# One 128-row load per image row, or two of 63 and 64 rows: the neighbourhood tiles of an involution and ternary convolution block

## The chip, the cores and the metric

The kernel runs on one core of one Trainium2 chip. The metric is the device time of a run in microseconds. Each time given for a kernel is the median of its runs; the kernel before has 2163.08 us as the median of three runs (2159.76 to 2169.76).

## The reference

The input x is 8 images of 256 channels, 56 x 56, in float32. Two layers follow, each added to its input.

```
x = x + involution(group_norm(x))      # 7x7 kernels made from x itself, 16 groups
x = x + block(group_norm(x))           # two 3x3 ternary convolutions, batch norms, ReLU

involution:  ker = w_span @ (w_reduce @ x + b_reduce) + b_span     # 16 x 49 per pixel
             out[c, y, x] = sum over 49 taps of ker[group(c), tap, y, x] * x_padded[c, y + i, x + j]
block:       out1 = relu(bn(conv(x, q1) + center));  out2 = bn(conv(out1, q2) + center)
             relu(out1 + out2),   q = weights quantized to -1, 0, 1
```

The change is in the involution, in the loads of the padded x that the 49 taps are taken from.

## The kernel before, in words

The kernel works in three stages. The first (to about 1043 us) is the involution with its group norm, the second (to about 1880 us) is the two convolutions, and the third is the closing pass over the results. The change is in the first.

In the first stage the 256 channels are split into four quarters of 64, and the image into an upper and a lower half, so that 128 partitions hold 64 channels of both halves. An image quarter is worked through in ten rows (TY = 10); a row is three image lines (the last one: one line) of seven tiles of 8 pixels. So there are 8 x 4 x 10 = 320 rows, and the stage is a list of them, in one order.

For each row there is a neighbourhood tile q. The host lays the padded image out in x_nb so that, for each quarter, one line of 896 values (3584 bytes: seven tiles by 128 channel halves) belongs to one position of a window of 9 x 14 = 126 positions (NQ). q holds 128 such lines, one per partition; 126 of them are read.

- `load_q` (L726) takes a buffer of the pool q (NQB = 5 buffers) and issues the load on SP, from 128 lines of x_nb in one DMA (L729).
- `fill_rim` (L746, its operation recorded at L752) adds the group's mean at the rim of the padded image, on POOL.
- `fill_end` (L761, L765) overwrites the lines below the image, on ACT, in the last two rows of a quarter.
- `apply_row` (L836, L853) multiplies q, on TensorE, by the matrices a that `generate` made for this quarter: 56 small matmuls (28 in the last row), out into the PSUM tile pa, which has two buffers.
- `pick_out` scales pa into inv on ACT (L863) and DVE (L865), and adds inv to x on POOL (L869).

Between the rows stand the pieces of the next quarter's `generate` (matmuls L821, ACT L825, DVE L829), the loads of the next image (`load_x`, L611), the stores of finished quarters (`store_x1`, L890), the statistics (L150), and the quantization of the convolution weights, which loads pieces (L221, L296) and stores planes (L325). All of these DMAs are issued on SP, in the order of the text.

Order: row i runs `apply_row`, then `prefetch` issues the load of row i + 5 (its buffer has just been read for the last time), then come the statistics and `pick_out`, then `surround` runs `fill_rim` of row i + 3 and `fill_end` of row i + 2. So a load has two rows until its rim is filled, and five until it is read. The function `pin` fixes the order of the text on each engine within the first stage. The second stage isn't pinned: its first instructions (the loads raw at L353 and wq at L342, the normalization xp at L1050 and L1052, the planes p, q, r, u, v at L388 to L416, the casts pl at L393) are placed by the scheduler of the framework, also among the last rows of the first stage. The convolution matmuls are at L523. The framework also gives each DMA one of eight semaphores in turn, and puts in the waits.

Of the kernel before, what the change touches and what calls it, by code (L numbers as in the profile page):

```python
# [17 lines left out]
P = 128  # L18
# [17 lines left out]
PY, PX = 3, 8  # L36
# [4 lines left out]
QY, QX = PY + K - 1, PX + K - 1  # L41
# [6 lines left out]
HQ = TY * PY + K - 1  # L48
# [42 lines left out]
def involution_tri_block_kernel(  # L91
# [3 lines left out]
    nc = tc.nc  # L95
# [484 lines left out]
    with ExitStack() as ph1:  # L580
# [121 lines left out]
        for j in range(2):  # L702
            o = j * nf // 2
# [22 lines left out]
        def load_q(b, c, ty):  # L726

            q = qpool.tile([P, TX, P], F32, tag="q", name=f"q_{b}_{c}_{ty}")
            nc.sync.dma_start(q.rearrange("p k c -> p (k c)"),  # L729
                              x_nb[b, c, (HQ - QY - PY * ty) * QX:(HQ - QY - PY * ty) * QX + P, :])  # L730
            return q

        def rim_of(b, c):
# [141 lines left out]
        def prefetch():  # L875
            if queue:
                k = queue.pop(0)
                loads[k] = load_q(*k)
                bare.append(k)
# [200 lines left out]
    with ExitStack() as ph4:  # L1080
# [10 lines left out]
        for j in range(B * CT):  # L1091
            b, t = j // CT, j % CT
# [98 lines left out]
```

## Time and profile before

| | us |
|---|---|
| median of three runs | 2163.08 |
| lowest, highest | 2159.76, 2169.76 |
| the profiled execution | 2159.04 |
| its span, from first to last instruction | 2157.3 |

The page's busy shares and its 40 slices (54 us each; a digit is the busy share in tenths):

```profile
PE 1748.1 (81%) x29680; PEld 1619.6 (75%) x29680; DVE 1751.9 (81%) x3337; ACT 1436.7 (67%) x3553; POOL 588.1 (27%) x965
...
PE   4898898989989898998799999997999999960000
...
DVE  5787878787777878777799999998999999984444
ACT  3877686877868787787366666665666666653344
POOL 0565565555556656566200000000000000000000
...
DMA  5667678686767768577633333335323333369999
```

The first 19 or 20 slices are the involution: all five engines and the DMA engines work side by side. The middle is the convolutions, with TensorE and DVE nearly full, and the last five are the closing pass, which moves data. The busiest DMAs by the page, with what each moves and the time from issue to landing (the last number, in us):

```profile
q<-in_x_nb SPq DMA_DIRECT2D x320, 448.0 KB, 4.1
...
x<-in_x SPq DMA_DIRECT2D x64, 392.0 KB, 5.2
x1d<-x SPq DMA_DIRECT2D x64, 392.0 KB, 5.3
```

### The profile page before, as it was taken

To read this page: it belongs to the slowest core of one execution; us is meant where nothing else is said; L and a number is where in the kernel's file an instruction comes from. 1 tells how busy PE (TensorE), PEld (TensorE's weight loads), DVE (VectorE), ACT (ScalarE), POOL (GpSimd) and SP (SyncE) were. 2 spreads that over 40 slices of the span, in tenths; PEclk is the share of its full clock that TensorE was granted. 3 is DMA by queue.
4 is the path that set the end of the run, shared out by engine and by line. 5 is a ranking of instruction groups with operands and counts; after the bars stand their busy time and mean duration, and the time that the engine had idled before them with its cause. 6 is when DMAs were issued, how large, how long until landed. Compare 5 with 4: busy or idle time off the path is not lost.

```text
span 2157.3 us, 70705 instructions
## 1 busy us (share of the span) xinstructions
PE 1748.1 (81%) x29680; PEld 1619.6 (75%) x29680; DVE 1751.9 (81%) x3337; ACT 1436.7 (67%) x3553; POOL 588.1 (27%) x965
## 2 busy tenths in 40 slices
PE   4898898989989898998799999997999999960000
PEld 4777786867777687876699999997999999960000
DVE  5787878787777878777799999998999999984444
ACT  3877686877868787787366666665666666653344
POOL 0565565555556656566200000000000000000000
PEclk9999899999999999999799999998999999985555
DMA  5667678686767768577633333335323333369999
GB/s 184 219 189 235 191 220 244 182 261 187 252 193 223 240 181 272 176 206 215 235 122 122 122 122 122 122 122 204 116 108 126 127 127 127 123 261 426 429 428 395
DMA packets 156250, 440.06 MB, mean 204 GB/s; under 512 B 63774, under 2 KB 74012, under 8 KB 148508
## 3 DMA queue, kind: packets, MB, share of 16 engines
q1 hardware_dynamic: 150336, 405.50, 55.3%
q10 hardware_dynamic: 5596, 30.03, 3.4%
q8 instruction: 235, 3.85, 0.7%
q14 instruction: 83, 0.68, 0.1%
HBM read 323.28 MB, written 112.20 MB: 202 GB/s over the span
## 4 chain that ended last, share of the span: by engine, by line
PE 69%; DMA 10%; issue 7%; DVE 6%; POOL 5%; ACT 3%; SPq 0%; ACTq 0%; POOLq 0%; DVEq 0%
PE c L523 40%; PE pg L821 15%; PE pa L853 9%; DMA x1f<-x1d 4%; PE pk L714 3%; DMA y1f<-y1d 3%; POOL q L752 2%; DMA out_y<-x1f 2%; POOL x L869 2%; PE ks L787 1%; ACT a L825 1%; DVE x1f L1103 1%; POOL x L801 1%; DVE a L829 1%; DMA sums<-in_w_all 1%
## 5 line engine op out<-in xcount | busy, mean ns | idle before, releaser
L523 PE MATMUL c<-pl,wq 128*128 128x392 f32 x4608 | 857.3, 349 | 14.4 <-ACT pl L393 14.4
L523 PEld LDWEIGHTS c<-pl,wq 128*128 128x128 f32 x4608 | 855.4, 190 | 16.1 <-ACT pl L393 14.8
L825 ACT ACTIVATE a<-pg,bt 126x126 f32<-126x126 f32 (+1 forms) x2048 | 537.4, 474 | 95.5 <-PE pg L821 94.0
L821 PE MATMUL pg<-kr,wl 64*126 64x140 f32 (+1 forms) x6144 | 464.8, 295 | 27.7 <-issue 13.2
L821 PEld LDWEIGHTS pg<-kr,wl 64*126 64x126 f32 x6144 | 401.4, 197 | 55.9 <-issue 19.0
L853 PE MATMUL pa<-a,q 126*32 126x48 f32 x17024 | 291.8, 214 | 80.4 <-issue 70.4
L853 PEld LDWEIGHTS pa<-a,q 126*32 126x32 f32 x17024 | 240.2, 115 | 148.2 <-issue 99.8
L829 DVE TENSOR_TENSOR a<-pg,bt 126x504 f32<-126x504 f32 (+4 forms) x640 | 282.3, 480 | 43.3 <-PE pg L821 41.9
L869 POOL TENSOR_TENSOR x<-x,inv 128x168 f32<-128x168 f32 x320 | 166.0, 519 | 403.5 <-DVE inv L865 357.5
L865 DVE SCALAR_TENSOR_TENSOR inv<-pa,gn1s,inv 128x168 f32<-128x168 f32 (+1 forms) x384 | 134.6, 351 | 167.0 <-ACT inv L863 163.3
L393 ACT CAST pl<-r 128x812 fp32r<-128x812 f32 x192 | 162.3, 868 | 142.8 <-DVE r L388 123.7
L373 POOL MEMSET xp<- 128x116 f32 x32 | 6.3, 195 | 825.7 <-DVE a L388 825.7
L752 POOL TENSOR_TENSOR q<-q,sides 126x256 f32<-126x256 f32 (+1 forms) x320 | 224.9, 703 | 2.1 <-PE pa L853 1.7
L394 DVE TENSOR_TENSOR pl<-r,pl 128x812 fp32r<-128x812 f32 x192 | 186.6, 998 | 29.9 <-ACT pl L393 28.6
L458 ACT ACTIVATE dummy<-y,nc 128x1568 f32<-128x1568 f32 (+1 forms) x128 | 200.2, 1564 | 4.8 <-DVE y L543 3.5
L863 ACT ACTIVATE inv<-pa,gn1s 128x168 f32<-128x168 f32 x320 | 135.5, 424 | 72.7 <-PE pa L853 53.8
L150 DVE BATCH_NORM_STATS2 st<-x 128x6 f32<-128x392 f32 x256 | 137.8, 554 | 10.4 <-DMA x<-in_x 9.4
L801 POOL TENSOR_TENSOR x<-x,add 128x504 f32<-128x504 f32 (+1 forms) x128 | 126.3, 1017 | 24.1 <-ACT add L795 24.1
L1050 ACT ACTIVATE xp<-raw,gn 128x392 f32<-128x392 f32 (+1 forms) x124 | 82.5, 721 | 61.3 <-DVE a L388 58.8
L1070 ACT ACTIVATE xp<-raw,bi_bn,sc_bn 128x392 f32<-128x392 f32 (+1 forms) x124 | 82.3, 721 | 58.8 <-DVE a L388 57.1
L1101 DVE SCALAR_TENSOR_TENSOR y1f<-y2f,sc_bn,y1f 128x3136 f32<-128x3136 f32 (+2 forms) x20 | 56.6, 2831 | 63.9 <-DMA y2f<-y2d 49.4
L714 PE MATMUL pk<-x,wrn 64*128 64x168 f32 (+1 forms) x1152 | 99.1, 312 | 2.1 <-issue 2.1
(174 smaller groups left out, 1776.7 us busy)
## 6 DMA issues: line engine op xcount, KB each, us to landing
q<-in_x_nb SPq DMA_DIRECT2D x320, 448.0 KB, 4.1
raw<-x1d SPq DMA_DIRECT2D x32, 812.0 KB, 6.1
raw<-y1d SPq DMA_DIRECT2D x32, 812.0 KB, 7.1
x<-in_x SPq DMA_DIRECT2D x64, 392.0 KB, 5.2
x1d<-x SPq DMA_DIRECT2D x64, 392.0 KB, 5.3
y1d<-y SPq DMA_DIRECT2D x30, 784.0 KB, 3.8
y2d<-y SPq DMA_DIRECT2D x30, 784.0 KB, 3.4
y1f<-y1d SPq DMA_DIRECT2D x14, 1568.0 KB, 15.1
```

Of the source, the lines that this page charges most:

```text
L393: nc.scalar.copy(hi, r)
L394: nc.vector.tensor_tensor(lo, r, hi.bitcast(F32), ALU.subtract)
L458: nc.scalar.activation(dst, v, f, bias=shift[:, to:to + 1], accum_out=stats[:, to, j, n:n + 1])
L523: nc.tensor.matmul(ps[:, to, :NM], wq[k][:, t, dx, to * P:(to + 1) * P], part[:, t, :, dx:dx + W], start=(c == 0), stop=(c == last))
L714: nc.tensor.matmul(ps[h][:, :m * W], wrn[rows, c, :], src[rows, r0:r0 + (m - 1) * PY + 1:PY, :], start=(c == 0), stop=(c == NCQ - 1))
L752: nc.gpsimd.tensor_tensor(v, v, z, ALU.add)
L801: nc.gpsimd.tensor_tensor(x_, x_, v, ALU.add)
L821: nc.tensor.matmul(dst, wl[rows, c, gp, o:o + NQ], kr[py][rows, px, :], start=True, stop=True)
L825: nc.scalar.activation(dst[:, g + 1, p0 + j], ps[1][:NQ, j * nt + t0:j * nt + t1], AF.Identity, bias=bt[:, c, g + 1, p0 + j:p0 + j + 1])
L829: nc.vector.tensor_tensor(dst[:, g, p0:p0 + n].rearrange("q p t -> q t p"), ps[0][:NQ, t0 * n:t1 * n].rearrange("q (t p) -> q t p", p=n), ...
L853: nc.tensor.matmul(ps[o:o + m, k * w:(k + 1) * w], q[:NQ, k, o:o + m], av[:, t + k, g * w:(g + 1) * w], start=True, stop=True)
L869: nc.gpsimd.tensor_tensor(xv, xv, iv.rearrange("p t (y x) -> p y t x", x=PX), ALU.add)
```

## The change

The load of a neighbourhood tile is issued as two DMAs, one behind the other on SP: the first brings lines 0 to 62 to partitions 0 to 62, the second lines 63 to 126 to partitions 63 to 126. Line 127, which was loaded before and which no instruction reads, is no longer loaded. Everything else in the text is the same.

```diff
         def load_q(b, c, ty):
 
             q = qpool.tile([P, TX, P], F32, tag="q", name=f"q_{b}_{c}_{ty}")
-            nc.sync.dma_start(q.rearrange("p k c -> p (k c)"),
-                              x_nb[b, c, (HQ - QY - PY * ty) * QX:(HQ - QY - PY * ty) * QX + P, :])
+            o = (HQ - QY - PY * ty) * QX
+            for p0, p1 in ((0, 63), (63, 127)):
+                nc.sync.dma_start(q[p0:p1].rearrange("p k c -> p (k c)"), x_nb[b, c, o + p0:o + p1, :])
             return q
 
```

## The prediction

> **What bounds the kernel now.** I read the page's busy shares and slices first, then the two stages by windows, the waits of the first stage, the DMA queues, what waits on the q loads, and the row-by-row timeline of the seam between the stages. All q loads lie in the first 1043 us; the rest is the convolutions (1043 to 1880 us) and the closing pass, which the diff doesn't touch. The first stage by windows, and the DMA queues in the same window:
>
> ```profile
> 60.00:1040.00 980.00, 856.53 (x24622) 732.81 (x24622) 763.55 (x2119) 751.08 (x2656) 576.08 (x919) 0.95 0.72 218
> ```
> ```profile
> DMA packets 119967, 213.75 MB, mean 218 GB/s; under 512 B 58336, under 2 KB 68064, under 8 KB 119714
> ...
> q8 instruction: 194, 3.18, 1.4%
> ...
> q<-in_x_nb SPq DMA_DIRECT2D x315, 448.0 KB, 4.1
> ```
>
> Columns of the first: window, length, busy us of PE, PEld, DVE, ACT, POOL, TensorE clock, DMA share, GB/s. TensorE works 857 of 980 us (87%); DVE and ACT follow at 78% and 77%; the DMA engines are busy 72% of the time. A row takes 980/315 = 3.1 us. What makes up TensorE's 123 idle us is in the waits of this window:
>
> ```profile
> PE pa L853 <- issue: 70.4, 66, 3.0
> ...
> PE pg L821 <- issue: 13.2, 12, 3.0
> ...
> PE pa L853 <- POOL q L752: 6.1, 2, 5.7
> ```
>
> The reader is to see that 70.4 + 13.2 = 84 us in 78 waits have no semaphore behind them ("issue"). In the trace's packet records most of these gaps end 1.2 to 1.6 us after the end of a 16,384-byte packet of the instruction queue (for example a packet at 602.20 to 603.09 us, matmuls again at 604.67). I read them as TensorE waiting for its own instructions[...]. Waits for q itself are 6 us, in two places. The q loads' own view in this window, what their first reader on POOL (L752) waited for, and SP's waits over the whole span:
>
> ```profile
> DMA to landing us min/median/max: 3.0/4.1/6.8
> ```
> ```profile
>   DMA q<-in_x_nb: 0.3, 1
> ```
> ```profile
> SPq L729 <- PE pa L853: 658.8, 301, 34.6
> ```
>
> One wait of 0.3 us in 320 rows: the loads are hidden. SP, which issues them, idles 659 us until TensorE frees a buffer. The seam is different:
>
> ```profile
> 1037.52 0.72 POOL L752 TENSOR_TENSOR q<-q,sides 126x256 f32<-126x256 f32 x1 [1.72 <-PE pa L853]
> ...
> 1038.28 0.56 ACT L765 COPY q<-low 70x448 f32<-70x448 f32 x1 [1.88 <-POOL q L752]
> ...
> 1039.66 2.99 PE L853 MATMUL pa<-a,q 126*32 126x48 f32 x84 [2.26 <-POOL x L869]
> ...
> 1040.70 1.75 DVE L1052 TENSOR_SCALAR xp<-raw,gn 128x392 f32<-128x392 f32 x4
> ...
> 1044.41 0.57 DVE L150 BATCH_NORM_STATS2 st<-x 128x6 f32<-128x392 f32 x1 [0.41 <-POOL x L869]
> ...
> 1051.26 1.00 DVE L415 TENSOR_TENSOR u<-xp 128x812 f32<-128x812 f32 x1
> ```
>
> The last q load lands at 1037.36 by the trace's landing records and POOL takes it at 1037.52: there the load is on the path.
>
> [...] Of before's DMAs 824 of 826 show 16 landing increments[...]; none here has 63 rows. [...] the x loads (128 partitions, 392 KB) land in 5.2 us, the x1 stores (64 partitions, 392 KB) in 5.3. [...]
>
> **The change part by part.**
>
> *Bytes.* Row 127, which nothing reads (the kernel uses 126), is dropped: 1/128 of the load. Nothing.
>
> *Engine shares.* [...] q is 315 x 448 KB = 145 of 214 MB, two thirds. [...]
>
> *When q lands.* An undisturbed q packet takes 0.14 us in the packet records. [...] the second issue adds its 0.33 us if the engines are otherwise free. Against that one disturbed row: a small transfer issued right behind q (0.38 us later) stalls on SP by 0.24 to 0.48 us on average, by up to 2.1 us at worst. Estimate from these: +0.7 us typically, +2 in bursts. The cover: by the landing records, the fill at L752 starts 4.3 us after landing at the median (1.2 at the lowest fiftieth), and TensorE reads the row another 5.2 us after the fill (median; 0.7 at least). Added row by row, 2 us makes 19 fills late by 14 us in all, and none reaches TensorE; nor does 3 us. Cost on the path: 0. Without this cover the 320 rows would cost 0.7 us each, 224 us.
>
> *SP.* 320 more issues of 0.33 us and 0.27 us of stalls each, some 190 us, out of 659 idle. What is queued behind each: the next x loads, x1 stores and weight pieces, all early by microseconds. The program has eight DMA semaphores in turn, so each issue waits for the landing of the eighth DMA before it. Before, the nearest of these is 2.0 us clear; with the halves counted, I find some 20 issues held back, 13 us in all, never over 2.3: again inside the cover. 0.
>
> *TensorE's waits.* Each row's first matmul waits for both halves. In the built program TensorE has 975 instructions that only wait, in place of 803, and POOL 548 in place of 388. One takes 51 ns on TensorE's sequencer (L853): 172 x 51 ns = 8.8 us at most. But the sequencer runs ahead: at 606.71 it handles the wait of a row whose matmuls start at 607.77. It costs only where the sequencer is late, 78 of 320 rows or fewer: between 0 and 8.8, I take 1 us. POOL's 160 at 17 ns are inside its idle 40%.
>
> *The seam.* The last load's landing passes through L752 (0.72), the copy at L765 (0.56), and the scaling ops queued behind it on ACT and DVE to the last three rows: +0.7 us. Past it, the built program's order differs. Before, four xp ops on DVE (1.75 us) stand ahead of the last two rows' ops; now they stand among and behind them, and u (1.00 us) stands ahead of the r that ACT and then TensorE wait for. Two xp ops between the last row's three (0.88), one behind the statistics (0.44), and u (1.00): +2.3 us before the first convolution matmul (1050.47 before). From there TensorE is the bound, so it stays. Between 0 (DVE waits hide it) and 3.5; I take 3.0 for landing and order together.
>
> *Instruction fetch.* The unknown. Fetches take 1.4% x 16 x 980 / 194 = 1.13 us each, the quickest tenth 0.90[...]. [...] No trace shows which engine it is. I take 0 and keep both ends.
>
> Sum: 1 + 3 = +4 us on the profiled execution's 2159.0 (span 2157.3 and 1.7 around it), 2163. The runs' median is 2163.1, 4 above that execution; on it, 2167.
>
> **The rivals.**
>
> *Slower by the fuller engines.* [...] each of the 78 waits grows by 0.2 us: +16, with the seam 2183; with all fetches +39, 2206. It decides from 0.09 us per wait, where 7 + 4 us pass 0.5%. For it: [...] 84 us already lost there. Against: half of the fetches run near their quickest time.
>
> *Faster by the emptier engines.* The same coin's other side: -16 + 4 gives 2151. [...] Against: other engines (ACT 77%, DVE 78%) soon hold TensorE.
>
> *The loads don't spread.* Were the 63 rows on one engine, 63 x 0.14 = 8.8 us per row against a pitch of 3.1: 320 x 5.7 us more, near 4000. [...]
>
> *SP's stalls* reach TensorE only from some 5 us per load; a row in ten late by 1 us would be +32, 2199.
>
> **How the numbers follow.** About 0.5%, 11 us, is what a measurement of this kernel can tell from no change. Forecast (hidden, +4): 0.60, 2157 to 2174. Fuller engines: 0.24, nearly all slower. Emptier: 0.12, most of it faster. Not spread: 0.02. SP: 0.02. Faster 0.12, same 0.61, slower 0.27. The range 2150 to 2192 leaves out the far end of the fuller engines' case and the last two.
>
> **What would show it.** Right: q's landing median (last half) 4.6 to 5.2 us; L752 waits for DMA under 15 us in all; TensorE's "issue" waits at L853 and L821 still 70 to 100 us; the first convolution matmul 2 to 5 us later. The fuller engines: mean fetch above 1.3 us and "issue" waits above 100; the emptier: below 1.05 and 70. The forecast is wrong if "PE pa <- POOL q" grows past 20 us, or if the landings double.

## The result and the profile after

The changed kernel takes 2190.1 us (median of four runs, 2180.8 to 2194.8), the kernel before beside it 2165.2: a ratio of 1.0111, 95% interval 1.0068 to 1.0153. On another chip, with 16 runs, it is 2178.8 against 2160.5, ratio 1.0081 (1.0062 to 1.0101). So the change costs 18 to 25 us. That is inside the predicted range, but +4 was forecast, and what the prediction called likeliest (no difference that can be measured) did not happen.

From the page of the changed kernel (the load now stands at L731, and what follows it one line lower than before), profiled in an execution of 2188.5 us:

```profile
span 2186.3 us, 71399 instructions
...
PE 1761.0 (81%) x29680; PEld 1631.5 (75%) x29680; DVE 1747.8 (80%) x3337; ACT 1438.5 (66%) x3553; POOL 589.2 (27%) x965
...
q8 instruction: 235, 3.85, 0.7%
...
L753 POOL TENSOR_TENSOR q<-q,sides 126x256 f32<-126x256 f32 (+1 forms) x320 | 225.2, 704 | 23.8 <-DMA q<-in_x_nb 17.5
```

DVE, ACT and POOL did the same work in the same time, but TensorE was busy for 1761 us where it had 1748, with the same 29680 matmuls. POOL's fill at L753 now does wait for its loads. The first stage by windows, then TensorE's and POOL's waits in it (pg is the PSUM tile of `generate`), then SP's over the whole span:

```profile
60.00:1060.00 1000.00, 865.42 (x24424) 740.01 (x24428) 756.97 (x2113) 748.60 (x2651) 571.65 (x911) 0.94 0.74 210
```
```profile
PE pa L854 <- issue: 65.8, 56, 4.6
...
PE pg L822 <- issue: 27.5, 15, 3.6
...
POOL q L753 <- DMA q<-in_x_nb: 25.3, 20, 2.6
...
PE pa L854 <- POOL q L753: 6.6, 2, 5.6
```
```profile
SPq L731 <- PE pa L854: 450.2, 257, 34.1
```

The reader is to see three things. POOL waits 25 us for q, in 20 places, but what reaches TensorE through "POOL q" is the same 6.6 us as before (6.1). "Issue", which I read as TensorE's wait for its instructions, is 93 us in sum where it was 84, in fewer and longer waits. And SP still has 450 us to spare.

Although so little comes through "POOL q", the loads no longer stay off the path. The page's chain of work that ended last (followed back from the last instruction, at each step to what released it), by engine, first before, then changed:

```profile
PE 69%; DMA 10%; issue 7%; DVE 6%; POOL 5%; ACT 3%; SPq 0%; ACTq 0%; POOLq 0%; DVEq 0%
```
```profile
PE 64%; DMA 13%; issue 10%; POOL 7%; DVE 5%; ACT 2%; SPq 0%; POOLq 0%; ACTq 0%; DVEq 0%
```

Within the first stage this chain goes through loads of q for 59 us in the changed kernel and 9 us in a second profile of it; before, for 4 us and, in its second profile, for none. The chain counts a load from its issue to its landing, so these times are not the loss itself.

Nearly all of the loss is in the first stage. From the first to the last row's scaling on ACT it lasts 1008.1 us; before, 980.7 in its first profile and 983.2 in a second. Everything behind that is 1114.7 us, against 1114.5 and 1115.4. Split up, with a second profile of either kernel (us, differences to the mean of the two profiles of before):

| first stage | before, two profiles | after | after, again |
|---|---|---|---|
| length | 980.7, 983.2 | 1008.1 (+26.1) | 990.1 (+8.1) |
| TensorE busy | 857.1, 857.4 | 868.6 (+11.4) | 859.4 (+2.2) |
| TensorE idle, "issue" | 86.6, 85.2 | 94.0 (+8.1) | 88.8 (+2.9) |
| TensorE idle, all else | 37.0, 40.6 | 45.5 (+6.7) | 41.9 (+3.1) |
| time at half clock | 109, 109 | 140 | 126 |

(A half-clock stretch that begins in the stage is counted to its end, which adds 11 to 13 us to every figure.) So the time went in parts of like size. Of "all else" after the change, 4.7 and 5.0 us are one wait for DVE's scaling just ahead of the last row; before has a gap of 3.5 and 5.0 us at that place, of which 1.3 and 5.0 are booked under "issue". The two profiled executions of the changed kernel (on two chips) differ by 18 us in this stage, those of before by 2.5. Two profiles of each are few: in all, 45 runs of before on one chip lie between 2146 and 2177 us, 16 of the changed kernel on that chip between 2169 and 2186.

The busy part goes with the clock: at the full clock a matmul of this stage stands for 33 to 34 ns of busy time in both kernels, at half clock for 51 to 58. Windows of the changed kernel, each the length of one slot of the clock's records (in both kernels every stretch of this stage between two changes lasts a whole number of 3.41 us; columns as in the windows above, the clock is the third number from the end):

```profile
89.70:93.10 3.40, 3.40 (x142) 3.13 (x131) 2.72 (x7) 3.40 (x18) 3.40 (x5) 1.00 0.84 238
93.10:96.50 3.40, 1.22 (x60) 0.85 (x58) 3.29 (x12) 1.80 (x10) 1.17 (x3) 1.00 0.88 282
96.50:99.90 3.40, 3.40 (x57) 3.13 (x49) 3.40 (x10) 2.33 (x10) 2.37 (x6) 0.51 0.89 289
99.90:103.30 3.40, 2.01 (x76) 1.69 (x72) 2.81 (x9) 1.38 (x6) 1.75 (x4) 0.99 0.78 219
```

In the second window TensorE stood still for 2.2 of 3.4 us; in the third it gets half the clock and does 57 matmuls in the time of 142. There are 26 such half-clock stretches in the stage (24 in the second profile), before 21 and 18. All 26 follow a slot in which TensorE was busy for at most 63% of the time, and every slot at full clock that was busy for less than 46% was followed by one. In the 14 profiles of this document together the two figures are 76% and 46%; in between, both happen. In 15 and 13 of the changed kernel's slots ahead of a stretch most of the idle time is behind an instruction fetch (before 10 and 12); in the others TensorE waits most often for ACT's copies at L826 or for the statistics (L166), and a wait for q takes part in one of either profile. In the second window above a slot that was busy for 36% was enough. Its stall of 2.2 us was paid for once more in the third, by some 1.5 us (an estimate: the third window's 57 matmuls, at the 33 ns of the full clock, would be 1.9 of its 3.4 us).

### The profile page after: what moved, and what is told of

The parts are those of the page before. It is cut to its first block, busy times and chain, and to the rows that moved or that the text cites. A ratio compares the mean times of both kernels' runs of the same rounds, so it can differ in the third digit from the quotient of the medians.

```text
span 2186.3 us, 71399 instructions
## 1 busy us (share of the span) xinstructions
PE 1761.0 (81%) x29680; PEld 1631.5 (75%) x29680; DVE 1747.8 (80%) x3337; ACT 1438.5 (66%) x3553; POOL 589.2 (27%) x965
## 2 busy tenths in 40 slices
DMA packets 158813, 438.95 MB, mean 201 GB/s; under 512 B 66654, under 2 KB 76892, under 8 KB 151068
## 4 chain that ended last, share of the span: by engine, by line
PE 64%; DMA 13%; issue 10%; POOL 7%; DVE 5%; ACT 2%; SPq 0%; POOLq 0%; ACTq 0%; DVEq 0%
PE c L523 39%; PE pg L822 12%; PE pa L854 7%; DMA q<-in_x_nb 3%; POOL q L753 3%; PE pk L714 3%; DMA y1f<-y1d 3%; DMA out_y<-x1f 3%; DMA y2f<-y2d 2%; POOL x L802 2%; PE ks L788 1%; POOL x L870 1%; DVE x1f L1104 1%; DMA x1f<-x1d 1%; ACT a L826 1%
## 5 line engine op out<-in xcount | busy, mean ns | idle before, releaser
L826 ACT ACTIVATE a<-pg,bt 126x126 f32<-126x126 f32 (+1 forms) x2048 | 539.3, 476 | 115.0 <-PE pg L822 114.3
L822 PE MATMUL pg<-kr,wl 64*126 64x140 f32 (+1 forms) x6144 | 474.1, 298 | 42.5 <-issue 27.5
L822 PEld LDWEIGHTS pg<-kr,wl 64*126 64x126 f32 x6144 | 410.1, 200 | 71.4 <-issue 34.6
L753 POOL TENSOR_TENSOR q<-q,sides 126x256 f32<-126x256 f32 (+1 forms) x320 | 225.2, 704 | 23.8 <-DMA q<-in_x_nb 17.5
L394 DVE TENSOR_TENSOR pl<-r,pl 128x812 fp32r<-128x812 f32 x192 | 186.5, 996 | 27.4 <-ACT pl L393 26.1
```

The lines of the kernel that those rows point to most:

```text
L394: nc.vector.tensor_tensor(lo, r, hi.bitcast(F32), ALU.subtract)
L753: nc.gpsimd.tensor_tensor(v, v, z, ALU.add)
L822: nc.tensor.matmul(dst, wl[rows, c, gp, o:o + NQ], kr[py][rows, px, :], start=True, stop=True)
L826: nc.scalar.activation(dst[:, g + 1, p0 + j], ps[1][:NQ, j * nt + t0:j * nt + t1], AF.Identity, bias=bt[:, c, g + 1, p0 + j:p0 + j + 1])
```

## Experiments

The theories at the start: *late data* (the halves land too late for POOL's fill), *rows* (an instruction fetch waits behind q's rows in a DMA engine, longer in a fuller one), *second transfer* (issues, semaphores, waiting instructions). They are guesses of mine. For each kernel I took from the trace two things. The first is the stalls of TensorE behind a fetch: gaps over 0.3 us that end 1.0 to 1.75 us after an instruction packet, up to 1075 us. The second is the wait of a fetch, from the start of instruction 192 of a block of 256 to the start of the packet, in blocks with 169 to 224 matmuls and weight loads of L853. The 60,166 recorded TensorE instructions make the 235 packets at 256 to a packet. The place 192 is where the record meets the edge of a block: 65 of the 68 stalls before, and 58 of the 65 after the change, come at instruction 193 or 194, so they do belong to the fetches. In the table, ratio is to the kernel before on the same chip; the stage is the first one as above; times are in us. All but the ratio comes from one profiled execution of each kernel, and a mean wait, of some 116 fetches, is uncertain by about 0.15 us. Counted to the end of the stage and no further, the stalls are 80 us in the first profile of before, 115 with 126 lines, 88 with 63 + 63 and 138 with the 64-byte transfer, and within 1 us of the table elsewhere.

| kernel | ratio (95%) | stage | stalls behind fetches | wait of a fetch | half clock | POOL's fill waits for q |
|---|---|---|---|---|---|---|
| before | 1 | 980.7 | 83.7 | 2.32 | 109 | 0.3 |
| before again | 1.0001 (0.9983–1.0018) | 983.2 | 83.5 | 2.32 | 109 | 2.4 |
| changed | 1.0111 (1.0068–1.0153) | 1008.1 | 88.8 | 2.49 | 140 | 25.3 |
| changed again | 1.0081 (1.0062–1.0101) | 990.1 | 80.8 | 2.25 | 126 | 11.4 |
| 64 + 64 lines | 1.0222 (1.0193–1.0252) | 1028.1 | 115.0 | 2.73 | 154 | 10.2 |
| one of 126 lines | 1.0210 (1.0174–1.0245) | 1018.0 | 109.8 | 2.67 | 147 | 5.9 |
| 63 + 63 lines | 1.0294 (1.0257–1.0331) | 1041.2 | 85.3 | 2.40 | 191 | 80.1 |
| changed, later fill | 1.0154 (1.0131–1.0177) | 1009.0 | 73.7 | 2.00 | 154 | 2.5 |
| 112 + 16 lines | 1.0161 (1.0102–1.0220) | 1023.1 | 107.0 | 2.59 | 157 | 6.4 |
| before + a 64-byte transfer | 1.0302 (1.0243–1.0362) | 1044.3 | 133.2 | 3.05 | 126 | 7.9 |
| one of 112 lines | 1.0103 (1.0044–1.0161) | 1006.9 | 69.8 | 2.02 | 154 | 2.4 |
| one of 64 lines | 1.0130 (1.0088–1.0172) | 1014.8 | 22.2 | 1.12 | 307 | 0 |
| pieces, 6/7 of the bytes | 0.9929 (0.9901–0.9958) | 967.8 | 69.6 | 2.04 | 106 | 1.6 |
| weights stored flat | 1.0006 (0.9990–1.0023) | 973.0 | 79.4 | 2.18 | 109 | 1.8 |

**Even halves, one odd load, nine engines.** How a transfer is spread shows in its packets of four bytes. Before has 13,343 of them for 826 DMAs, 16 to each (but for 128 that are the data of b_red), and 824 of the DMAs show 16 landing increments. By the packets under 512 bytes (63,774 before) a load of 128 lines has 16 of them and so have loads of 112 (63,774), 64 (63,775) and 16 lines (68,894 with the 112 + 16), one of 126 lines has 14 (63,135), and one of 63 has 9 (66,654 in the changed kernel). I take each for the share of one of the 16 DMA engines that the page counts. That makes 8, 7, 4, 1, 9 and 7 rows to an engine. It is an estimate, since no packet in the trace names its engine; all numbers of rows and of engines below rest on it.

Three divisions of the load, in place of (0, 63), (63, 127): eight rows on each of 16 engines in two transfers; nine rows on 14 engines in one; fourteen rows on nine engines in two.

```diff
-            for p0, p1 in ((0, 63), (63, 127)):
+            for p0, p1 in ((0, 64), (64, 128)):
+            for p0, p1 in ((0, 126),):
+            for p0, p1 in ((0, 63), (63, 126)):
```

> Two transfers of 64 and 64 lines in place of 63 and 64[...], with the same number of DMAs and of waits as in the changed kernel. If the uneven load of the engines[...] makes the changed kernel slower: about 2165 us, within 6 of the kernel before. If the second DMA of each row, its issue on SP and the second wait on TensorE and POOL make it slower: about 2190 us, as the changed kernel.

> One transfer of 126 lines: [...] one DMA and one wait per row as before. Uneven load: [...] some +8 us, 2173. Number of DMAs and waits: 2165 us, no change. [...]

> Two transfers of 63 lines: [...] DMAs and waits as in the changed kernel. Uneven load: [...] at least twice the loss, +50 us or more, 2215 or above, with q landing later than in the changed kernel. Number of DMAs and waits: 2190 us, as the changed kernel.

The even halves should have been as fast as before if uneven engines were the cause; they lose about twice what the change loses. The single load of 126 lines, without any second transfer, loses as much, where the two theories had expected 8 us or none. So a load can cost that much without uneven engines, and without a second transfer. The waits of the first stage, first for the even halves, then for the 126 lines:

```profile
PE pa L854 <- issue: 69.6, 59, 5.0
...
PE pg L822 <- issue: 34.7, 21, 3.2
POOL q L753 <- DMA q<-in_x_nb: 10.2, 8, 2.8
```
```profile
PE pa L854 <- issue: 77.1, 59, 3.7
...
PE pg L822 <- issue: 27.1, 15, 4.6
```

Both have 104 us of "issue" where before has 84, and little late data. With fourteen rows on nine engines, which lose 66 us where the theory of uneven engines had asked for 50 or more, it is the other way round:

```profile
POOL q L753 <- DMA q<-in_x_nb: 80.1, 52, 3.7
PE pa L854 <- issue: 68.6, 48, 4.3
DVE piece_w L301 <- DMA piece_w<-in_w: 43.5, 17, 5.5
...
PE pg L822 <- issue: 19.3, 14, 3.4
```

Here POOL and DVE wait 124 us for data, "issue" is 88, and the chain that ended last goes through loads of q for 107 us of the stage. There are two routes, then: late data and late instructions.

**A later fill.** The change with one more row between the load and the fill of the rim, so that a late landing finds POOL later:

```diff
-PLEAD = 2
+PLEAD = 3
```

> The changed kernel with PLEAD = 3 in place of 2: POOL fills the rim one row later, so a load has three rows to land and the filled tile two rows until it is read. If the loss comes through POOL waiting for q (24 us of such waits in the changed kernel's trace): POOL's waits for q fall below 5 us and the time to 2165 to 2175 us. If it comes through TensorE's own stalls (instructions fetched later, and the lower clock after a stall): no change, 2185 to 2192 us.

Nothing is won, although POOL's fill waits 2.5 us in place of 25. TensorE's "issue" waits fall, but it now waits for the fill itself (before, 6 us):

```profile
PE pa L854 <- POOL q L753: 46.3, 36, 6.5
...
PE pa L854 <- issue: 44.0, 32, 4.0
```

This doesn't clear late data as a part of the loss, since the later fill took away slack behind it; it shows that the slack can't be moved at no cost.

**The second transfer.** The changed kernel again; the same eight rows per engine as seven and one; and the kernel before with a small transfer added, for which no row waits (its text is four lines longer, so that L857 and L825 in its waits are L853 and L821 of before):

```diff
-            for p0, p1 in ((0, 63), (63, 127)):
+            for p0, p1 in ((0, 112), (112, 128)):
```
```diff
+    note_d = [dram.tile([1, 16], F32, tag=f"note{i}", name=f"note{i}") for i in range(16)]
...
+            i = ((b * NCQ + c) * TY + ty) % 16
+            nc.sync.dma_start(note_d[i], x_nb[b, c, o:o + 1, :16])
```

> The changed kernel once more, beside three others on one chip. Every theory: a ratio of 1.011 to 1.016 to the kernel before, stage 1 (first row of applied matrices to last) some 25 to 35 us longer, the fetch of TensorE's instructions starting about 2.5 us after its block boundary.

> Two transfers, lines 0 to 112 and 112 to 128: [...] in two transfers as in the change. Second-transfer theory: as with the even split, a ratio of 1.015 to 1.025, SP's issues at over 500 ns. Fetch theory by rows alone: [...] 1.000 to 1.005. Late-data theory: the first 112 lines land as before, 16 rows follow at once, POOL waits for the loads under 8 us, 1.000 to 1.006.

> The kernel before, with a second transfer of one row of 64 bytes to a scratch tensor behind every neighbourhood load; nothing waits for it except, 16 loads later, the transfer that writes the same row again. It adds SP's second issue[...], and no waiting instruction on TensorE or POOL. Second-transfer theory, if the cost is the issue and the queue: 1.010 to 1.022. If the cost is in the waiting instructions or in the rows: 0.998 to 1.004. Fetch theory by rows: 1.000 to 1.003.

The changed kernel, once more, lost less than expected: 18 us, and 8 us of the stage in its profile. Seven and one costs 36 us, the even halves 48, so what comes second may be large or small. The 64-byte transfer costs most of all, 65 us, more than any theory had allowed it. The waits of the first stage with it:

```profile
PE pa L857 <- issue: 98.8, 70, 3.4
...
PE pg L825 <- issue: 28.2, 23, 2.6
POOL q L756 <- DMA q<-in_x_nb: 7.9, 10, 1.9
```

"Issue" is 127 us, 43 more than before, and data is hardly late. This kernel has 806 waiting instructions on TensorE (before 803) and 387 on POOL (388), so these aren't the cause of its loss; and the added bytes are none to speak of. The trace's records show what they became: over the whole execution 23,583 packets of four bytes instead of 13,343, which is 32 more for each of the 320 loads. That fits 16 pieces of 4 bytes for the data and 16 more packets, as many as the load of q itself has, and 315 of the small transfers do show 16 landing increments. Whether it is these packets that the next fetch waits for isn't shown: no run separates them from the other sides of a second transfer, such as the second issue on SP.

**Fewer rows.** One transfer of 112 lines (seven rows per engine), and of 64 (four); the products contract over as many lines. In the diff, n is 112 or 64:

```diff
+            nc.sync.dma_start(q[:n].rearrange("p k c -> p (k c)"), x_nb[b, c, o:o + n, :])
...
-                        nc.tensor.matmul(ps[o:o + m, k * w:(k + 1) * w], q[:NQ, k, o:o + m],
-                                         av[:, t + k, g * w:(g + 1) * w], start=True, stop=True)
+                        nc.tensor.matmul(ps[o:o + m, k * w:(k + 1) * w], q[:n, k, o:o + m],
+                                         av[:n, t + k, g * w:(g + 1) * w], start=True, stop=True)
```

> One transfer of 112 lines in place of 128[...]. It leaves 14 of the 126 neighbourhood lines out of the product (contraction over 112 lines); the instructions are otherwise the same. Fetch theory[...]: fewer rows ahead of it, so the packet starts under 2.2 us after its boundary (before 2.32), and stage 1 gets shorter by 15 to 45 us, ratio 0.980 to 0.993. Late-data theory (the neighbourhoods land too late): in before nothing was late (0.3 us of waits), so nothing is gained, ratio 0.998 to 1.002. Second-transfer theory (issue, semaphores, waits of one more DMA): no second transfer, 1.000.

> One transfer of 64 lines in place of 128[...]. It leaves 62 of the 126 neighbourhood lines out of the product (contraction over 64 lines); the instructions are otherwise the same. Theory that the fetch of TensorE's instructions waits behind the transfers under way: from eight rows to seven its stalls fell by 14 us and its wait by 0.30 us, so with four the wait before the packet is 1.0 to 1.5 us and the stalls are 20 to 45 us; if that sets the time, 2095 to 2125 us (ratio 0.970 to 0.984). If TensorE's clock and its waits for the other engines take the gain back, as with 112 lines, the stalls fall as said and the ratio is 1.000 to 1.010. Theory that the stalls have nothing to do with the loads: stalls of 75 to 92 us.

The products leave out 14 and 62 of the 126 lines. The fetches did what the rows theory says, to its numbers. With one transfer of 64, 112, 128 or 126 lines (four, seven, eight or nine rows to an engine) a fetch waits 1.12, 2.02, 2.32 and 2.67 us, and the stalls are 22, 70, 84 and 110 us. The steps from seven to eight and to nine rows are little more than the uncertainty of one mean; the whole range is far more. The time did not follow: both kernels are slower than before, with 112 lines by 1.0% where no theory had allowed more than 0.2, with 64 by 1.3% where the worst was 1.0. The waits of the first stage with 64 lines, and its windows over the whole stage and around one stall:

```profile
PE pa L853 <- issue: 29.3, 33, 3.3
PE pg L821 <- DVE a L829: 18.9, 6, 4.5
...
PE pg L821 <- issue: 3.0, 4, 1.2
```
```profile
60.00:1060.00 1000.00, 918.73 (x24306) 798.27 (x24302) 794.21 (x2110) 753.74 (x2654) 559.98 (x900) 0.86 0.52 138
```
```profile
621.50:624.90 3.40, 1.94 (x84) 1.62 (x71) 3.36 (x7) 2.70 (x10) 1.84 (x3) 1.00 0.94 231
624.90:628.30 3.40, 3.15 (x43) 3.04 (x45) 1.92 (x6) 1.24 (x4) 1.52 (x4) 0.50 0.30 82
628.30:638.60 10.30, 10.30 (x169) 7.31 (x171) 5.01 (x16) 6.10 (x17) 4.30 (x7) 0.50 0.27 68
638.60:652.20 13.60, 13.60 (x264) 12.37 (x256) 10.26 (x44) 8.56 (x38) 6.33 (x11) 0.50 0.38 100
652.20:655.60 3.40, 3.40 (x113) 3.12 (x105) 2.49 (x9) 2.17 (x10) 2.17 (x4) 1.00 0.85 181
```

TensorE hardly waits for instructions any more (32 us), yet is busy for 919 of 1000 us, at a mean clock of 0.86. After one short stall it ran 27 us at half clock although it was busy all along. The stage has 307 us of half clock in 23 stretches, before 109 in 21. What it gained in fetches it paid in clock. Why the clock stayed low so long isn't shown: the bytes, the shorter contraction and the other values that it computes came together here.

**Bytes or packets.** The kernel before, each line of q in two pieces of 1536 bytes, with the fourth of seven tiles left out, and the contraction whole; the fourth tile's products use the third. In the 32 rows that fill the top rim the fill takes one more small operation on POOL. With it ran the kernel before once more, for its second profile:

```diff
+            nc.sync.dma_start(bass.AP(q[:].tensor, q[:].offset, [q[:].ap[0], [4 * P, 2], [1, 3 * P]]),
+                              bass.AP(halves.tensor, halves.offset, [halves.ap[0], [4 * P, 2], [1, 3 * P]]))
...
-                        nc.tensor.matmul(ps[o:o + m, k * w:(k + 1) * w], q[:NQ, k, o:o + m],
+                        nc.tensor.matmul(ps[o:o + m, k * w:(k + 1) * w], q[:NQ, k - (k == 3), o:o + m],
```

> One transfer of 128 lines, but each line in two pieces of 1536 bytes with the fourth tile of each line left out (its products use the third): [...] six sevenths of the bytes, no second transfer. If what the fetch waits for is the number of packets ahead of it: 0.3 us a packet, the packet starts over 4 us after its boundary and the ratio is over 1.05. If it is bytes: as with seven rows, a wait of 1.9 to 2.2 us, stalls of 60 to 80 us, ratio 0.995 to 1.010. If it is the number of transfers: as in before, stalls of 75 to 92 us, 0.998 to 1.005.

> The kernel before once more, for a second profile of it. Every theory: ratio 0.998 to 1.002, stage 1 of 975 to 990 us, stalls of TensorE behind instruction fetches of 75 to 92 us (83.7 in the first profile).

Twice the packets, and the fetch waits less: 2.04 us and 69.6 us of stalls, the values of seven rows (a sixteenth of this load is 16 x 1536 bytes, the bytes of 6.9 rows). Had each packet cost a fetch its share of before, the wait would have been over 4 us; so within a transfer it isn't the number of packets, and bytes fit. And this time the time follows: the median falls by 16 us to 2142.0 where the stalls fall by 14, a ratio just below the expected range. Its waits, and its windows:

```profile
PE pa L856 <- issue: 59.8, 52, 4.8
```
```profile
60.00:1060.00 1000.00, 878.26 (x24827) 754.31 (x24824) 794.44 (x2173) 765.93 (x2686) 579.71 (x954) 0.95 0.67 201
```

Beside the 112 lines, with the same fetches, half clock is 106 us and not 154, and over all runs the mean clock is 0.916 to 0.920 against 0.905 to 0.911. The two kernels differ in the contraction (126 lines or 112), in 2% of the bytes, in the size of the packets, in POOL's fill and in the values that they compute. That the shorter contraction lowers the clock would fit both kernels that have it, but no run changes it alone.

**A way to be faster?** If transfers under way delay fetches, fewer packets in the stage's other transfers might help. The quantised weights stored flat, 128 packets of 1152 bytes instead of 768 of 192. The 12 loads that bring them back for the convolutions then read pieces of 192 bytes, and land 8.8 us after their issue at the median where before it was 5.0:

```diff
-                bass.AP(dst[:].tensor, dst[:].offset + o,
-                        [[QS * CT * 3 * C, P], [CT * 3 * C, QS], [1, QN]]),
+            nc.sync.dma_start(dst[:, k * QS * QN:(k + 1) * QS * QN], held.pop(k)[:, 4 * QN:])
...
-        nc.sync.dma_start(w.rearrange("p t k o -> p (t k o)").bitcast(F32),
-                          wq_d[i - 1][:, SLOT[k] * n:(SLOT[k] + 1) * n])
+        v = wq_d[i - 1].rearrange("p (j s n) -> p s j n", s=QS, n=QN)
+        nc.sync.dma_start(w.rearrange("p t k o -> p (t k o)").bitcast(F32).rearrange(
+            "p (j n) -> p j n", n=QN), v[:, SLOT[k]])
```

> The kernel before, with the quantised weights written to the scratch tensor as one piece of 1152 bytes a partition (128 packets a transfer) and not as six of 192 (768 packets); the 12 later loads of the weights read 192-byte pieces instead. Whole computation. Theory that the fetch waits behind transfers under way: the 60 or so fetches that meet such a store start up to 0.6 us sooner, stage 1 gets 0 to 20 us shorter; the first loads of the convolution stage are 0 to 6 us later; ratio 0.992 to 1.002. If these stores don't matter: 1.000 to 1.004.

No gain, 1.0006. The stage is 973 us in the profile, 8 to 10 less than before, but that execution took 2155.0 us, 7 less than the kernel's median of 2162.5, so its short stage isn't shown to be the kernel's. No kernel that does the whole computation was faster than before.

## Where the prediction held and where it missed, step by step

*Engine shares.* 318 of the 320 transfers of 63 lines show ten landing increments (319 in the second profile): nine as the data lands, and one about 0.5 us after the issue, ahead of all data (0.47 us at the median, where the next comes at 3.34). The transfers of 64 lines show 16 (318 of 320). If increments, like the packets of four bytes, are engines, and the nine are among the 16, nine engines got eleven rows of a load and seven got four. The DMA share of the stage rose from 0.72 to 0.74, far from full.

*When q lands.* A little short at the median, and short in the tail. From the first issue to the last landing it is 5.4 us at the median (5.0 in the second profile, 4.1 before), where I said 4.6 to 5.2; and the slowest tenth begins at 8.2 (5.8 before), 2.4 later, where I allowed 2 us in bursts. The worst is 12.1 (11.0 before). Hence 25.3 us of waits on POOL in the first profile, where I had said under 15 (11.4 in the second). TensorE's own wait for POOL's q stayed at 6.6, under the 20 that would have refuted the forecast; but that sign was too narrow, since the chain that ended last goes through these loads for 59 and 9 us of the stage.

*SP.* The second of two issues in a row takes 0.52 us, the first 0.28, where a single one takes 0.33, but 450 of 659 us of idle are left. Nothing on the path, as forecast.

*TensorE's and POOL's extra waits.* No run isolates them. The 64-byte transfer, without them, costs more than the change with them, so a loss of this size doesn't need them; what they add is not shown.

*The seam.* Forecast +3, measured about +1. TensorE's gap ahead of the last row is 4.7 and 5.0 us, now a wait for DVE's scaling, in before 1.3 + 2.3 and, in the second profile, 5.0. From the last row's scaling to the first convolution matmul it is 8.5 us in both profiles, before 7.7 in both; and from there to the end it is no longer than before. Most of the order's 2.3 us was absorbed.

*Instruction fetch.* Taken at 0 between -16 and +39; in sum the stalls changed by +5 and by -3, and "issue" stayed between the 70 and 100 us that I had named. I had priced the packet's own duration, which hardly moved (1.11 and 1.07 us before, 1.13 and 1.12 after); what moves between the kernels is the wait ahead of it, which the prediction didn't look at. So the 0 came out nearly right by luck. Averaged by their turn in eight (12 to 17 fetches to a turn, waits over 8 us left out, each mean uncertain by some 0.4 us), the waits lie between 1.8 and 2.8 us in both profiles of before, but between 1.2 and 4.3 in the changed kernel (1.4 and 3.4 in its second profile; 1.2 and 4.9 with 63 + 63 lines). So some turns waited longer than in before and some shorter, and the sum stayed. That these are the fuller and the emptier engines of the two rivals isn't shown, since no packet in the trace names its engine. With 64 + 64 and with 112 + 16 lines the turns lie between 2.1 and 3.3 us: none falls below the least of before, and the stalls grow by 31 and 23 us (with 126 lines by 26, with the 64-byte transfer by 50). In no kernel here that computes the whole are the fetches hidden: TensorE's stalls behind them are 74 to 133 us.

*The step that failed* is the sum: "1 + 3 = +4 us". It took TensorE's busy time as fixed, let no other wait grow, and had the loads' "cost on the path: 0". In their place stand +11 and +2 us of busy time at a lower clock, +8 and +3 of "issue", +7 and +3 of all other waits, and loads of q that the chain does go through. The cover that I computed row by row from the landings of before, with 2 or 3 us added to each, was right about the one wait of TensorE for the fill, and blind to the slower tail of the landings and to what a stall does to the clock afterwards. That the range held the result is in part luck: its upper end stood for a longer fetch packet, and the loss came another way. More than half of the changed kernel's half-clock stretches follow a fetch's stall, but which part of the 18 to 25 us is late data and which late instructions stays open.

## What to carry to other kernels

In this stage TensorE runs some 50 instructions a microsecond (24,622 matmuls and as many weight loads in 980 us) beside DMA engines that are busy for 72% of the time, and lost 84 of 980 us to "issue". In one like it, compare "issue" waits before and after any change of the transfers, even of ones that no engine waits for. Here one more transfer per step cost more than its bytes (64 bytes, 3.0%), and one load of 128 lines was 2.1% faster than one of 126, although nobody reads the last two. A stall of 2.2 us cost some 1.5 us more, by estimate, where the clock dropped after it, so a change that looks hidden is to be judged by TensorE's busy time too, not by its waits alone.

## What was not expected of the hardware

- A transfer of 64 bytes added to each row's load made the kernel 65 us slower (3.0%), with the wait of an instruction fetch up from 2.32 to 3.05 us.
- Within one transfer the number of packets didn't set the fetch's wait: with 256 packets of 1536 bytes to a load it is 2.04 us, with 112 of 3584 it is 2.02.
- Half clock didn't need an idle slot: in all 14 profiles every 3.4 us slot at full clock in which TensorE was busy for less than 46% was followed by one at half clock.
- Halving the bytes of the loads took 61 of 84 us of fetch stalls away, and the kernel was slower by 1.3%, because TensorE then spent 307 us at half clock instead of 109.
